# Transposition by VectorE squares and DRAM instead of DMA transposition, and three more products of halves, in a graph network on one Trainium2 core

## The chip, the core and the metric

The kernel runs on one core of a Trainium2 chip. A core has a matrix engine (TensorE, in the profile PE, its weight loads PEld), a vector engine (VectorE, DVE), a scalar engine (ScalarE, ACT), a general engine (GpSimd, POOL) and a queue that issues DMAs (SyncE, SP). The engines run side by side, each through its own instructions in their order, and wait for one another through semaphores. The metric is the device time of one execution in microseconds.

## What is computed

64 graphs of 256 nodes with 256 features each go through two layers. The first is two graph attentions, a norm, a feed forward of 1024 hidden units with relu and a norm; the second is an attention of 8 heads with one value projection for each value of adj, a norm, a feed forward with gelu and a norm. Cut to what matters:

```python
def gat(h, adj, W, a):                       # twice, W1/a1 and W2/a2
    Wh = h @ W
    e = leaky_relu(Wh @ a[:F] + swapaxes(Wh @ a[F:], 1, 2), 0.2)
    return softmax(where(adj > 0, e, -9e15), axis=1) @ Wh
h = layernorm(x + gat(gat(x, adj, W1, a1), adj, W2, a2))
h = layernorm(h + relu(h @ w_ff1 + b_ff1) @ w_ff2 + b_ff2)
q, k = heads(h @ Wq + bq), heads(h @ Wk + bk)
attn = softmax(q @ k.T / sqrt(32))
out = sum(attn * (adj == r) @ heads(h @ Wv[r] + bv[r]) for r in range(4))
x = layernorm(h + out @ Wo + bo)
return layernorm(x + gelu(x @ W1 + b1) @ W2 + b2)
```

adj holds 0 and 1. The kernel relies on it: it looks at all of adj on the way, and a general version at the end runs only if another value was seen.

## The kernel before

All numbers are float32. A matmul of float32 shows in the profile as two records. The work on one graph is cut into pieces with names such as `F.hk1` or `A.dt10`. The letter ahead of the dot is the stage: L loads, G the two graph attentions and the sum with x, F the first feed forward and the projections, A the attention, T its end, the second feed forward and the store. Three lists written out by hand in the file, `START`, `PERIOD` and `END` (lines 43, 65 and 106), set the order of all pieces. `PERIOD` names every piece once with a lag: in the period of graph b, piece `A.pm00/4` works on graph b - 4. So up to six graphs are under way at once, in a loop that repeats 59 times. The order within an engine is the order of this list; the tile pools and the semaphores add the waits. The DMAs of the loop are all issued by SP, in the order of the list too.

Products are made in two ways. `seven_products` (line 598) multiplies a 2x2 arrangement of blocks with seven block products instead of eight, with differences of the weight blocks made in setup (`half_factors`, line 245) and sums of the left blocks (`add_sums`, line 577, on POOL). Its pieces a to e are matmuls, k1 to k4 evict a block from PSUM, p1 to p3 add a further block to it on DVE (line 638). Both feed forwards' first products, the values v and the second feed forward's second product (line 703, tile fX_c, fY_c, fZ_c) are made so. The first feed forward's second product (`out`, line 683, tile ff_a) and q and k (`project`, line 835) are made the plain way, with eight matmuls of 256 columns for each half of the nodes or features; q and k are evicted by ACT with their bias (line 849).

A tile that is to be multiplied from the other side must be transposed: the normed features y of three norms, and the attention p of each of the 8 heads. `turned` (line 462) does it with the DMA's transposition, which takes 16 bit elements. `dt` issues a DMA transposition of the tile seen as halves of float32 (line 470), `dm` two plain DMAs that bring the halves together on the right partitions (line 478), and `mg` a copy by ACT, or for two of the heads by POOL, that interleaves the 16 bit halves to float32 again (line 485). The results are cols and pm. So y and p are written in an order that suits this (lines 520 and 898).

Elsewhere DVE takes part as follows. `away` (line 740) makes the mask of absent edges from adj; line 743 takes adj's maximum for the look at its values. Line 798 multiplies the projected features by the inverse sums of the softmax (whz). Line 926 masks pm. Line 503 adds the residual at the head of a norm, among others to ff_a. Lines 530 and 537 finish the last norm (res_d). POOL scales p by the inverse sums of the softmax (line 911), makes the roots of the norms (line 515), the residuals (lines 555 and 562) and the sums of blocks (line 585).

Of the kernel before, what the change touches and what calls it, by code (L numbers as in the profile page):

```python
# [43 lines left out]
T.hk3/5 A.ex12/3 F.f0/2 A.mx10/3 T.hd/5 A.pm00/4 G.rsA/1 A.vk4/4 L.xT/0 A.mg02/4 A.dm03/4 T.hp3/5  # L44
F.f1/2 T.raC/5 A.ex10/3 G.nmA/1 T.hp2/5 A.pm02/4 A.mg03/4 A.rz12/3 G.wh0/0 T.he/5 T.ge0/5 L.adj/0
A.pm01/4 T.ge1/5 G.wc0/0 A.sp13/3 A.dt11/3 F.dtA/1 A.pm03/4 T.rbC/5 F.lnB/2 A.sp12/3 A.dm11/3
T.hk4/5 A.dt13/3 A.pm12/4 A.rz10/3 G.wh1/0 T.ge2/5 A.sc0/3 F.rsB/2 A.mx02/3 A.o0/4 F.dmA/1 T.ge3/5
G.wc1/0 F.nmB/2 A.sp10/3 F.raA/1 A.o1/4 A.mx03/3 T.u0/5 A.mx01/3 T.fa/5 A.dt12/3 A.mx00/3 A.ex02/3
A.dm13/3 L.x/0 A.oc0/4 A.oc1/4 F.cA/1 F.dtB/2 T.wo/4 A.dt10/3 G.away/0 G.eA/0 T.u1/5 T.u3/5
A.ex03/3 A.ex01/3 G.lrA/0 F.sA/1 T.fk1/5 F.dmB/2 T.fp1/5 T.fb/5 A.mg11/3 F.ha/1 A.dm10/3 T.lnC/4  # L50
F.hb/1 T.fk2/5 G.adA/0 A.rz03/3 A.rz01/3 T.fc/5 T.rsC/4 T.u2/5 F.hk1/1 F.hk2/1 A.sp01/3 T.nmC/4
F.hc/1 T.fk3/5 F.hp1/1 A.ex00/3 G.exA/0 F.hk3/1 A.va/3 T.dtC/4 A.mg13/3 A.rz02/3 F.cB/2 G.rzA/0
T.fp3/5 A.pm11/3 F.hp3/1 T.fd/5 A.sp02/3 G.gA0/0 F.hd/1 G.wd0/0 F.raB/3 T.fp2/5 A.mg10/3 A.rz00/3
G.gA1/0 A.sp00/3 F.hp2/1 A.vk1/3 T.fe/5 T.fk4/5 A.vb/3 A.vk2/3 G.wd1/0 T.lnD/5 A.pm13/3 F.r0/1
F.he/1 A.dt01/3 G.eB/0 F.k/2 F.q/2 A.vp1/3 F.r1/1 T.dmC/4 G.lrB/0 T.cC/4 A.dm12/3 G.adB/0 F.ke0/2
F.hk4/1 F.ke1/2 A.vc/3 A.vk3/3 A.sp03/3 T.sC/4 A.dm01/3 T.ha/4 F.qe0/2 F.qe1/2 G.exB/0 A.dt00/3
A.dt02/3 T.hk1/4 A.vp3/3 A.sc1/2 T.hb/4 A.vd/3 T.nmD/5 G.rzB/0 F.r2/1 T.hp1/4 A.mx11/2 A.mg01/3
A.mx13/2 A.dt03/3 T.rsD/5 F.rbB/3 A.dm00/3 G.gB/0 T.hk2/4 A.vp2/3 A.pm10/3 T.rbD/5 A.mx12/2 F.r3/1
A.ex11/2 F.rbA/1 A.mg12/3 A.rz11/2 A.dm02/3 G.lnA/0 A.ex13/2 F.sB/2 A.mg00/3 T.out/5 A.rz13/2
A.ve/3 A.sp11/2 T.hc/4  # L60
# [5 lines left out]
G.wh0:0 G.wh1:0 G.wc0:0 L.xT:1 G.away:0 G.wc1:0 G.eA:0 G.lrA:0 S.f0:0 G.adA:0 G.exA:0 G.rzA:0  # L66
G.gA0:0 G.wd0:0 G.gA1:0 G.wd1:0 G.eB:0 G.wh1:1 G.lrB:0 L.adj:1 G.wh0:1 S.f1:0 G.adB:0 G.exB:0
G.wc0:1 G.wc1:1 G.rzB:0 L.xT:2 G.gB:0 G.eA:1 G.away:1 G.lrA:1 S.v0:0 G.lnA:0 G.rsA:0 G.nmA:0
G.adA:1 G.wh0:2 S.f2:0 G.exA:1 L.adj:2 G.rzA:1 F.dtA:0 F.dmA:0 S.q0:0 G.wh1:2 G.gA1:1 S.lw:0
G.gA0:1 G.wc0:2 S.v1:0 G.wd0:1 S.q1:0 G.wd1:1 S.v2:0 F.cA:0 F.sA:0 G.eB:1 F.ha:0 G.lrB:1 F.hk1:0  # L70
S.j1:0 F.hb:0 F.raA:0 F.hk2:0 L.x:1 F.hc:0 F.hk3:0 F.hd:0 G.adB:1 S.lr:0 F.hp3:0 F.hp2:0 S.v3:0
G.exB:1 G.wc1:2 F.r0:0 L.xT:3 G.wh0:3 G.rzB:1 F.he:0 F.r1:0 G.eA:2 F.hp1:0 G.away:2 F.hk4:0
F.rbA:0 F.r2:0 G.gB:1 L.adj:3 G.lnA:1 G.rsA:1 F.r3:0 G.nmA:1 G.lrA:2 F.f0:0 F.f1:0 G.adA:2 F.lnB:0
G.wc0:3 F.rsB:0 G.exA:2 F.dtA:1 G.wh1:3 F.dmA:1 S.l0:0 F.nmB:0 G.rzA:2 F.dtB:0 F.cA:1 G.gA1:2
F.ha:1 G.gA0:2 F.sA:1 F.hb:1 F.hk1:1 F.hk2:1 G.wd0:2 G.wd1:2 F.dmB:0 F.hc:1 G.away:3 F.cB:0 G.eB:2
F.k:0 S.l1:0 G.lrB:2 F.hk3:1 F.ke0:0 L.xT:4 F.hp1:1 F.ke1:0 S.l2:0 F.q:0 F.hd:1 G.wc1:3 G.eA:3
G.adB:2 F.qe0:0 F.hp3:1 F.qe1:0 F.hp2:1 A.sc1:0 G.exB:2 F.he:1 F.r0:1 G.rzB:2 F.r1:1 A.mx10:0
A.ex10:0 A.mx11:0 S.p2:0 S.j2:0 A.ex11:0 F.hk4:1 A.mx12:0 A.rz10:0 A.ex12:0 F.sB:0 F.r2:1 L.x:2
G.gB:2 F.r3:1 A.sc0:0 G.lnA:2 A.mx02:0 A.rz11:0 G.lrA:3 A.sp10:0 A.rz12:0 A.dt10:0 G.rsA:2 G.nmA:2
A.mx00:0 G.adA:3 A.sp11:0 A.mx13:0 F.dtA:2 G.exA:3 F.f0:1 F.raA:1 A.dm10:0 A.dt11:0 A.ex02:0  # L80
F.rbA:1 F.dmA:2 G.rzA:3 A.ex13:0 A.ex00:0 F.cA:2 A.sp12:0 F.f1:1 A.dt12:0 A.rz02:0 A.dm11:0
F.lnB:1 G.gA0:3 G.wd0:3 G.gA1:3 A.mg10:0 G.wh0:4 A.mx01:0 F.rsB:1 G.wc0:4 G.wh1:4 A.vb:0 A.rz13:0
A.sp02:0 A.ex01:0 G.wc1:4 F.nmB:1 L.x:3 G.wd1:3 A.dm12:0 F.sA:2 A.mg11:0 A.rz00:0 F.dtB:1 A.sp00:0
A.dt02:0 F.dmB:1 A.va:0 A.mx03:0 A.vk1:0 A.vk2:0 F.ha:2 F.hk1:2 G.eB:3 F.hb:2 F.hk2:2 A.mg12:0
F.hc:2 A.vc:0 A.dt00:0 A.ex03:0 A.sp13:0 F.hk3:2 F.cB:1 F.hp1:2 A.dm00:0 A.pm10:0 A.rz01:0 F.hd:2
A.dm02:0 A.pm11:0 F.k:1 A.vp1:0 F.hp2:2 F.hp3:2 G.lrB:3 A.vk3:0 F.raA:2 A.dt13:0 A.rz03:0 F.r0:2
F.raB:1 F.r1:2 F.ke0:1 F.q:1 G.adB:3 A.sp01:0 F.qe0:1 A.vp3:0 F.rbB:1 A.vd:0 A.sp03:0 F.ke1:1
L.adj:4 A.dt03:0 F.he:2 A.dt01:0 F.qe1:1 A.vp2:0 G.exB:3 A.pm12:0 G.rzB:3 A.ve:0 F.hk4:2 A.sc1:1
A.mg00:0 A.mx13:1 F.r2:2 A.mx11:1 A.dm03:0 F.rbA:2 F.r3:2 A.ex13:1 A.vk4:0 G.gB:3 A.pm00:0
A.dm01:0 A.mg02:0 A.ex11:1 A.mx10:1 A.dm13:0 A.ex10:1 A.mg03:0 A.rz13:1 G.lnA:3 F.raB:0 A.sp13:1  # L90
A.mg01:0 G.rsA:3 A.mx12:1 A.mg13:0 A.rz11:1 A.rz10:1 G.nmA:3 F.f0:2 A.sc0:1 G.eA:4 A.dt13:1
A.ex12:1 A.pm02:0 A.mx01:1 G.lrA:4 A.sp10:1 F.dtA:3 A.mx03:1 A.pm01:0 A.ex03:1 A.pm03:0 F.f1:2
A.o0:0 A.pm13:0 F.lnB:2 A.rz12:1 F.rbB:0 A.dt10:1 G.away:4 A.ex01:1 A.oc0:0 A.rz03:1 A.o1:0
F.dmA:3 A.va:1 A.oc1:0 A.sp11:1 A.dm13:1 F.rsB:2 A.sp12:1 F.nmB:2 T.wo:0 F.cA:3 A.rz01:1 G.adA:4
A.vk1:1 F.ha:3 G.exA:4 A.dm10:1 F.hk1:3 A.vp1:1 T.lnC:0 F.sA:3 T.rsC:0 A.mx00:1 G.rzA:4 F.hb:3
A.mg10:1 F.hk2:3 T.nmC:0 F.dtB:2 F.hc:3 A.sp01:1 A.mg13:1 A.dt11:1 A.ex00:1 A.dt12:1 G.gA0:4
A.mx02:1 F.sB:1 F.hk3:3 F.dmB:2 F.cB:2 F.hp3:3 A.rz00:1 G.gA1:4 A.dm11:1 F.hd:3 G.wd0:4 A.sp00:1
A.ex02:1 F.hp1:3 G.wd1:4 F.k:2 F.raA:3 A.mg11:1 T.dtC:0 A.rz02:1 A.dm12:1 F.q:2 T.dmC:0 F.hp2:3
F.ke0:2 A.vb:1 F.ke1:2 G.eB:4 F.qe0:2 F.he:3 A.dt01:1 F.qe1:2 A.vk2:1 A.sc1:2 A.dt00:1 G.lrB:4
A.mx11:2 T.cC:0 F.rbA:3 F.hk4:3 G.adB:4 A.ex11:2 A.vc:1 A.sp02:1 F.r0:3 A.mx13:2 T.ha:0 A.vk3:1  # L100
A.sp03:1 G.exB:4 F.r1:3 G.rzB:4 T.hk1:0 A.vp3:1 A.vd:1 A.dm01:1 A.dm00:1 A.ex13:2 A.vp2:1 T.sC:0
T.hb:0 T.hk2:0 A.dt02:1 L.x:4 F.r2:3 A.rz11:2 A.mg00:1 F.r3:3 A.mg12:1 G.gB:4 A.mx12:2 A.sp11:2
T.hp1:0 T.hc:0 A.dt03:1 A.pm10:1 G.lnA:4 A.pm11:1 A.mg01:1 A.ve:1 A.pm13:1 F.sB:2 A.rz13:2
A.dm02:1
""".split()
END = """
G.rsA:-1 A.vk4:-4 F.f0:-2 A.mx10:-3 T.hk3:-5 T.raC:-5 T.hp3:-5 A.dm03:-4 G.nmA:-1 A.pm00:-4
A.ex10:-3 T.hd:-5 T.hp2:-5 A.ex12:-3 A.sc0:-3 A.dt11:-3 A.mx02:-3 A.mg03:-4 A.sp13:-3 A.pm03:-4
A.mg02:-4 A.ex02:-3 A.pm12:-4 T.ge0:-5 F.dtA:-1 A.dt13:-3 T.he:-5 A.pm01:-4 A.pm02:-4 T.ge1:-5
F.f1:-2 F.dmA:-1 A.o0:-4 A.rz12:-3 T.hk4:-5 F.cA:-1 A.sp12:-3 T.ge2:-5 T.rbC:-5 A.oc0:-4 A.mx01:-3  # L110
F.lnB:-2 A.dm11:-3 A.o1:-4 F.rsB:-2 A.dm13:-3 F.sA:-1 A.rz02:-3 T.ge3:-5 F.ha:-1 A.sp02:-3
F.nmB:-2 A.oc1:-4 F.hb:-1 F.hk1:-1 F.raB:-3 A.rz10:-3 T.u0:-5 T.wo:-4 A.dt12:-3 A.mx00:-3
A.mg11:-3 F.hk2:-1 F.hc:-1 T.u2:-5 F.hp1:-1 A.mx03:-3 T.lnC:-4 F.dtB:-2 T.rsC:-4 T.u1:-5 T.nmC:-4
T.fb:-5 T.u3:-5 A.dt02:-3 A.ex01:-3 F.dmB:-2 T.fa:-5 A.ex00:-3 T.fk1:-5 F.hk3:-1 A.sp10:-3
A.ex03:-3 T.fk2:-5 F.cB:-2 F.hd:-1 A.va:-3 F.raA:-1 F.hp2:-1 A.rz01:-3 F.q:-2 A.dm02:-3 A.rz00:-3
F.hp3:-1 A.pm11:-3 A.sp00:-3 A.vk1:-3 T.fc:-5 A.mg02:-3 A.rz03:-3 F.qe0:-2 T.dtC:-4 T.fk3:-5
T.fp1:-5 F.r0:-1 F.k:-2 A.sp01:-3 T.fd:-5 F.qe1:-2 T.fp3:-5 A.mg13:-3 A.vp1:-3 F.ke0:-2 F.ke1:-2
T.fp2:-5 A.pm02:-3 F.he:-1 A.dm12:-3 A.dt10:-3 A.vb:-3 A.sc1:-2 A.sp03:-3 A.vk2:-3 F.r1:-1
T.dmC:-4 A.mx12:-2 T.cC:-4 F.hk4:-1 A.dm10:-3 A.dt00:-3 A.vc:-3 A.vk3:-3 A.vp3:-3 F.r2:-1
A.ex12:-2 F.rbA:-1 A.mx13:-2 T.fe:-5 A.mx11:-2 T.fk4:-5 A.rz12:-2 T.ha:-4 A.mg12:-3 T.sC:-4  # L120
A.dt03:-3 F.r3:-1 A.mg10:-3 A.mx10:-2 A.ex13:-2 A.ex10:-2 A.rz10:-2 F.rbB:-3 T.hk1:-4 A.dt01:-3
A.vd:-3 T.hb:-4 T.raC:-4 T.hk2:-4 A.dm00:-3 A.vp2:-3 A.pm10:-3 T.hp1:-4 F.f0:-1 A.sp12:-2 T.lnD:-5
A.mg00:-3 T.hc:-4 A.dm01:-3 A.ex11:-2 A.sc0:-2 T.hk3:-4 T.hd:-4 A.rz13:-2 A.dm03:-3 A.pm12:-3
A.sp10:-2 A.rz11:-2 A.pm13:-3 A.mg03:-3 A.ve:-3 A.sp11:-2 A.dt12:-2 A.mx01:-2 T.hp2:-4 T.hp3:-4
# [63 lines left out]
def binary(ctx: ExitStack, tc: tile.TileContext, t, most, out: bass.AP):  # L188
# [56 lines left out]
    def half_factors(name, width, block):  # L245
# [4 lines left out]
        for at, c, h in ((0, 0, 0), (5, 0, 1), (1, 1, 0), (2, 1, 1)):  # L250
            src = block(c, h)
            to = f[:, at, :]
            if len(src.shape) == 3:
                to = to.rearrange("p (f d) -> p f d", f=src.shape[1])
# [1064 lines left out]
```

## Time and profile before

| What | Value |
|---|---|
| median of three runs | 3073.11 us (3071.72 to 3075.26) |
| span of the profiled execution | 3073.1 us |
| PE busy | 97% of the span, 23270 records |
| DVE, ACT, POOL busy | 83%, 83%, 71% |
| share of the DMA engines in the middle of the run | 0.79, at 148 GB/s |
| TensorE clock granted | 0.994 of full speed in the mean |

The first line of the profile's page gives each engine's busy time. The chain of waits goes back from the last instruction to whatever released it, step by step. A line of the windows gives start and end of a stretch, its length, and then for PE, PEld, DVE, ACT and POOL the busy time and, in brackets, the number of instructions, last the granted clock, the share of the DMA engines and GB/s. A line of the timeline has start and length, then engine, line, operation and what is written from what. An instruction's length overlaps the start of the next one on its engine a little, so that work is better counted from start to start.

### The profile page before, as it was taken

The numbers are of one execution on the slowest core, as the hardware profiler recorded it, in microseconds if no ns is written. First come the engines' busy times: TensorE is split into PE (matmuls) and PEld (weight loads), VectorE is DVE, ScalarE is ACT, GpSimd is POOL, SyncE is SP. The second block draws the span as 40 slices with busy tenths as digits, with TensorE's granted clock in tenths as the row PEclk, the third lists the DMA queues.
The fourth block names the chain that finished last, engine by engine and source line by source line (L and its number), as shares of the span: only waits on it lengthen the run. The fifth ranks groups of instructions, "written<-read, shape, count | busy, mean of one in ns | idle before, by whom it ended". The sixth has DMA issues, their size and how long they took to land.

```text
span 3073.1 us, 68797 instructions
## 1 busy us (share of the span) xinstructions
PE 2985.9 (97%) x23270; PEld 2612.4 (85%) x23270; DVE 2539.8 (83%) x5740; ACT 2556.6 (83%) x5822; POOL 2176.7 (71%) x3057
## 2 busy tenths in 40 slices
PE   7999999999999999999999999999999999999996
PEld 6788888888888888888888888888888888888885
DVE  5788888888888888888888888888888888888865
ACT  2788888888888888888888888888888888888884
POOL 4777777777777777777767777777777777777675
PEclk9999999999999999999999999999999999999999
DMA  6787877879778788777867778878787788788794
GB/s 161 126 160 143 151 152 144 149 146 151 149 147 152 145 148 150 150 143 148 153 143 150 149 142 152 152 140 151 152 145 149 151 145 148 148 151 147 142 146 77
DMA packets 1023941, 449.40 MB, mean 146 GB/s; under 512 B 771008, under 2 KB 1021888, under 8 KB 1023584
## 3 DMA queue, kind: packets, MB, share of 16 engines
q1 hardware_dynamic: 1022048, 442.43, 77.0%
q8 instruction: 187, 3.06, 0.5%
q0 software_dynamic: 976, 1.72, 0.4%
q14 instruction: 170, 1.39, 0.2%
q10 hardware_dynamic: 560, 0.79, 0.1%
HBM read 58.87 MB, written 16.78 MB: 25 GB/s over the span
## 4 chain that ended last, share of the span: by engine, by line
PE 84%; DVE 11%; DMA 2%; issue 1%; ACT 1%; POOL 0%; SPq 0%; DVEq 0%; POOLq 0%; ACTq 0%
PE ff_a L687 14%; PE fX_c L703 7%; PE o L936 7%; PE hX_a L662 7%; PE hX_c L662 5%; DVE res_d L530 5%; PE gat_b L804 4%; PE gat_a L804 4%; PE k L839 4%; PE q L839 4%; PE hY_a L662 4%; PE wh L748 4%; PE fY_c L703 4%; PE wo L955 3%; PE vX L852 3%; PE sc L884 2%
## 5 line engine op out<-in xcount | busy, mean ns | idle before, releaser
L485 ACT COPY pm<-halves_p 128x1024 uint16<-128x1024 uint16 x384 | 520.1, 1357 | 43.2 <-DMA halves_p<-pairs_p 43.1
L687 PE MATMUL ff_a<-w_L_gnn_w_ff,hid_a 128*128 128x256 f32 x2048 | 463.0, 379 | 0.2 <-ACT hid_a L679 0.2
L687 PEld LDWEIGHTS ff_a<-w_L_gnn_w_ff,hid_a 128*128 128x128 f32 x2048 | 379.7, 190 | 47.3 <-ACT hid_a L679 0.6
L926 DVE SCALAR_TENSOR_TENSOR pm<-away,pm 128x512 f32<-128x512 uint8 x512 | 407.3, 806 | 3.7 <-ACT pm L485 2.5
L936 PE MATMUL o<-pm,v 128*32 128x256 f32 x4096 | 234.9, 381 | 0.7 <-DVE pm L926 0.7
L585 POOL TENSOR_TENSOR S_c<-cols_c 128x128 f32<-128x128 f32 x128 | 59.3, 463 | 246.1 <-ACT cols_c L485 246.1
L703 PEld LDWEIGHTS fX_c<-f_L_gnn_W,hid_c 128*128 128x128 f32 x1536 | 196.6, 192 | 35.8 <-ACT oT L947 23.9
L679 ACT ACTIVATE hid_a<-hid_a,col_L_gnn_b_ff 128x256 f32<-128x256 f32 x512 | 225.1, 503 | 0.1
L679 ACT ACTIVATE hid_c<-hid_c,col_L_gnn_b 128x256 f32<-128x256 f32 x512 | 218.5, 497 | 4.8 <-DVE hid_c L638 2.0
L703 PE MATMUL fX_c<-f_L_gnn_W,hid_c 128*128 128x128 f32 x1536 | 209.9, 280 | 3.2 <-ACT hid_c L679 1.6
L936 PEld LDWEIGHTS o<-pm,v 128*32 128x32 f32 x4096 | 126.2, 110 | 98.4 <-POOL rstd_b L515 18.9
L485 POOL COPY pm<-halves_p 128x1024 uint16<-128x1024 uint16 x128 | 172.4, 1347 | 12.8 <-DMA halves_p<-pairs_p 12.7
L530 DVE SCALAR_TENSOR_TENSOR res_d<-acc_c,mv_d,row_L_gnn_g 128x256 f32<-128x256 f32 x128 | 170.8, 1373 | 0.0
L804 PE MATMUL gat_b<-whz_B,s_B 128*128 128x256 f32 x512 | 127.3, 391 | 36.3 <-DVE hid_c L638 33.1
L804 PEld LDWEIGHTS gat_b<-whz_B,s_B 128*128 128x128 f32 x512 | 91.7, 189 | 71.0 <-DVE hid_c L638 56.8
L662 PEld LDWEIGHTS hX_c<-cols_c,f_L_gnn_W 128*128 128x128 f32 x1024 | 133.7, 191 | 17.4 <-ACT cols_c L485 8.0
L884 PE MATMUL sc<-kT,qT 32*128 32x256 f32 x2048 | 147.7, 400 | 0.0
L662 PE MATMUL hX_c<-cols_c,f_L_gnn_W 128*128 128x128 f32 x1024 | 135.9, 276 | 8.3 <-ACT cols_c L485 7.2
L662 PEld LDWEIGHTS hY_c<-S_c,f_L_gnn_W 128*128 128x128 f32 x1024 | 126.1, 193 | 19.9 <-issue 19.6
L662 PE MATMUL hY_c<-S_c,f_L_gnn_W 128*128 128x128 f32 x1024 | 142.7, 283 | 0.0
L804 PE MATMUL gat_a<-whz_A,s_A 128*128 128x258 f32 x512 | 137.3, 392 | 5.2 <-DVE whz_A L798 4.9
L662 PEld LDWEIGHTS hX_c<-S_c,f_L_gnn_W 128*128 128x128 f32 x1024 | 133.7, 191 | 9.2 <-ACT hid_c L673 2.1
(2758 smaller groups left out, 9567.5 us busy)
## 6 DMA issues: line engine op xcount, KB each, us to landing
halves_p<-pairs_p SPq DMA_DIRECT2D x1024, 128.0 KB, 3.3
xT<-in_xT SPq DMA_DIRECT2D x64, 256.0 KB, 3.3
adj<-in_adjT SPq DMA_DIRECT2D x64, 256.0 KB, 3.4
x<-in_x SPq DMA_DIRECT2D x64, 256.0 KB, 4.4
halves_y_a<-pairs_y_a SPq DMA_DIRECT2D x128, 128.0 KB, 3.5
halves_y_y<-pairs_y_y SPq DMA_DIRECT2D x128, 128.0 KB, 3.1
halves_y_c<-pairs_y_c SPq DMA_DIRECT2D x128, 128.0 KB, 3.2
out<-res_d SPq DMA_DIRECT2D x64, 256.0 KB, 2.2
```

The lines of the kernel that those rows point to most:

```text
L485: copy(into().bitcast(U16).rearrange("p (n s) -> p s n", s=2), t["halves"].rearrange("p s k q -> p s (k q)"),)
L530: nc.vector.scalar_tensor_tensor(tiles["res"][:, i, :], tiles["acc"][:, i, :], tiles["mv"][:, i, 0:1], rows[last[0]], ALU.subtract, ALU.mult,)
L662: nc.tensor.matmul(ps[:, f * P : (f + 1) * P], weights()[0][:, factor, f * P : (f + 1) * P], left, start=start and f == 0, stop=f == FC // ...
L679: nc.scalar.activation(tiles["hid"][:, f, :], tiles["hid"][:, f, :], func, bias=b1[:, f : f + 1])
L687: nc.tensor.matmul(tiles["ff"][:, i, :], tiles["hid"][:, f, nodes(i)], weights()[2][:, f, :], start=(f == 0), stop=(f == FC - 1),)
L703: nc.tensor.matmul(ps, left[:, f, :], weights()[2][:, factor, f * P : (f + 1) * P], start=start and f == 0, stop=f == FC // 2 - 1, skip_gr ...
L748: nc.tensor.matmul(t["whp", j], tiles["xT"][:, c, nodes(j)], wx[:, c, :], start=(c == 0), stop=(c == KC - 1),)
L804: nc.tensor.matmul(ps, t["s"][:, j, nodes(i)], t["whz"][:, j, :width], start=(j == 0), stop=(j == NT - 1),)
L839: nc.tensor.matmul(t[key + "p"][:, o, :], w[:, c, nodes(o)], tiles["cols"][:, c, :], start=(c == 0), stop=(c == KC - 1),)
L884: nc.tensor.matmul(t["sc", g, hh][:, i, :], qkv["q"][hd, g, nodes(i)], qkv["k"][hd, g, :], start=True, stop=True,)
L926: nc.vector.scalar_tensor_tensor(pm[:, 1, :], tiles["away"], 0.0, pm[:, 0, :], ALU.is_equal, ALU.mult)
L936: nc.tensor.matmul(ps[hh * DH : (hh + 1) * DH, :], qkv["v"][:, j, d0 : d0 + DH], t["pm", (g, hh)][:, r, j * N : (j + 1) * N], start=(r == ...
```

## The change

The change has several parts. It replaces the DMA transposition by DVE's transposition in squares of 32x32 float32 (`dt`), a plain DMA of the tile to DRAM (`dm`) and four plain DMAs back, one for each quarter of the partitions (`mg`); heads are handled in pairs, so that there are four tiles p of 1024 columns in place of eight of 512. The copies that joined halves are gone. The orders within y, p, pm, e, s, away, and of x and adj in DRAM follow from this. The first feed forward's second product becomes a `seven_products` like the second's, and q and k together become one. whz is multiplied on ACT. The look at adj becomes a square on ACT with a sum (of (2 adj - 1) squared, which is the number of entries if all are 0 or 1). The tiles pm have 4 buffers of double size. Weights are loaded in more pieces. And the three lists are new; `PERIOD` reaches to lag 6.

```diff
-    def turned(do, stage, key, name, src, into, engine):
+    def turned(do, stage, key, name, width, src, into, out=None):
...
-        def turn():
-            t["pairs"] = work.tile([P, 2, 4, P], U16, tag="pairs", name=f"pairs_{name}", bufs=3)
-            nc.sync.dma_start_transpose(
-                out=t["pairs"].rearrange("p c k q -> p (c k) q"),
-                in_=src().rearrange("p c a b n -> p (c a b n)").bitcast(U16),
-            )
+        def squares():
+            rows = src()
+            t["squares"], to = out() if out else (rows, rows)
+            nc.vector.transpose(to, rows)
+
+        def leave():
+            t["far"] = far.tile([4, 32, 4, width], F32, tag=f"far{width}", name=f"far_{name}", bufs=8)
+            nc.sync.dma_start(
+                out=t["far"].rearrange("a c b n -> (a c) (b n)"), in_=t["squares"]
+            )
 
-        def part():
-            t["halves"] = work.tile([P, 2, 4, P], U16, tag="halves", name=f"halves_{name}", bufs=3)
-            for c in range(2):
+        def back():
+            to = into()
+            for b in range(4):
                 nc.sync.dma_start(
-                    out=t["halves"][c * 64 : (c + 1) * 64].rearrange("p s k q -> p s (k q)"),
-                    in_=t["pairs"][:, c].rearrange("p k q -> p (k q)"),
-                )
-
-        def join():
-            copy = nc.scalar.copy if engine == "ACT" else nc.gpsimd.tensor_copy
-            copy(
-                into().bitcast(U16).rearrange("p (n s) -> p s n", s=2),
-                t["halves"].rearrange("p s k q -> p s (k q)"),
-            )
+                    out=to[b * 32 : (b + 1) * 32],
+                    in_=t["far"][:, :, b, :].rearrange("a c n -> c a n"),
+                )
...
         def into():
-            tiles["cols"] = work.tile([P, KC, N], F32, tag="cols", name=f"cols_{name}", bufs=3)
-            return tiles["cols"].rearrange("p k n -> p (k n)")
+            cols = work.tile([P, KC * N], F32, tag="cols", name=f"cols_{name}", bufs=3)
+            if pairs:
+                tiles["cols"] = cols.rearrange("p (n k) -> p k n", k=KC)
+            else:
+                tiles["cols"] = cols.rearrange("p (a t k r) -> p k t a r", a=4, t=NT, k=KC)
+            return cols.rearrange("p (a n) -> p a n", a=4)
...
-            nc.vector.tensor_reduce(most[:, b : b + 1], tiles["adj"].bitcast(U32), AX.X, ALU.max)
+        def binary_or_not():
+            nc.scalar.activation(
+                tiles["adj"], tiles["adj"], AF.Square, bias=minus_one, scale=2.0,
+                accum_out=most[:, b : b + 1],
+            )
...
-                nc.vector.tensor_scalar_mul(
-                    t["whz"][:, j, :width], t["wh", step][:, j, :width], rz[:, j : j + 1]
+                nc.scalar.activation(
+                    t["whz"][:, j, :width], t["wh", step][:, j, :width], AF.Copy,
+                    scale=rz[:, j : j + 1],
                 )
...
-        def project(w, key):
-            t[key + "p"] = mm_tile(f"{key}_{b}")
-            for o in range(KC):
-                for c in range(KC):
-                    nc.tensor.matmul(
-                        t[key + "p"][:, o, :], w[:, c, nodes(o)], tiles["cols"][:, c, :],
-                        start=(c == 0), stop=(c == KC - 1),
-                    )
+        def natural(ap):
+            return ap.rearrange("p (a t r) -> p t a r", a=2, t=NT)
+
+        def into(ps, factor, left, start):
+            for n, (w, right) in enumerate(((wq, natural(left)), (wk, left))):
+                nc.tensor.matmul(
+                    ps[:, nodes(n)], w[:, factor, :], right,
+                    start=start and n == 0, stop=n == 1, skip_group_check=True,
+                )
...
+        def begin_keys(i, h, ps):
+            for to, src, bias in zip(keys(i, h), both(ps), (bq, bk)):
+                nc.scalar.activation(to, src, AF.Identity, bias=bias[:, h : h + 1])
+
+        def add_keys(i, h, ps):
+            for to, src in zip(keys(i, h), both(ps)):
+                nc.vector.tensor_tensor(to, to, src, ALU.add)
...
-        feed_forward(do, "F", f"a{b}", a, lambda: ff0, "r", AF.Relu, seven=False)
-        y = layernorm(do, "F", "B", f"b{b}", lambda: (a["ff"], a["res"]))
-        to_columns(do, "F", "B", f"y{b}", y, "ACT")
+        feed_forward(do, "F", f"a{b}", a, lambda: ff0, "r", AF.Relu)
+        y = layernorm(do, "F", "B", f"b{b}", lambda: (a["ff"],))
+        to_columns(do, "F", "B", f"y{b}", y, pairs=True)
```

`far` is a pool in DRAM with 8 buffers of each size. In the order of the built program, one period holds 39 DMAs on SP: 7 stores to DRAM, 28 loads from it, and those of x, its transpose, adj and the output.

## The prediction

> **What bounds the kernel now.** I read the page's first part, then a table of windows for the steady stretch, then the chain of waits.
>
> ```profile
> span 3073.1 us, 68797 instructions
> PE 2985.9 (97%) x23270; PEld 2612.4 (85%) x23270; DVE 2539.8 (83%) x5740; ACT 2556.6 (83%) x5822; POOL 2176.7 (71%) x3057
> ...
> PE 84%; DVE 11%; DMA 2%; issue 1%; ACT 1%; POOL 0%; SPq 0%; DVEq 0%; POOLq 0%; ACTq 0%
> ```
>
> TensorE (PE) carries the chain. In the chain's list the same pieces come back every 46.494 us (the output products of attention at 320.35, 366.85 and 413.35), so 64 graphs take 64 x 46.494 = 2975.6 and filling, draining and setup the other 97.5. The profiled span, 3073.1, equals the median of the runs, 3073.11, so no correction is needed between them.
>
> The window holds fifty periods (start and length; busy PE, weight loads, VectorE, ScalarE, GpSimd):
>
> ```profile
> 325.40:2650.00 2324.60, 2296.54 (x18101) 2016.21 (x18100) 1974.71 (x4451) 1999.63 (x4551) 1670.50 (x2351) 1.00 0.79 148
> ```
>
> Per period: PE 45.93 of 46.49, VectorE (DVE) 39.49, ScalarE (ACT) 39.99, GpSimd (POOL) 33.41; the granted clock is 1.00. PE idles 0.56. Where, the chain in order of time shows (start, length, who):
>
> ```profile
> 1006.24 3.46 PE ff_a L687 x16
> 1009.70 0.89 PE hX_c L662 x8
> ...
> 1039.26 1.73 PE k L839 x8
> 1040.99 1.73 PE q L839 x8
> 1042.72 0.45 PE vX L852 x2
> ...
> 1043.72 0.42 DVE v L638
> 1044.14 2.72 DVE res_d L530 x2
> ```
>
> Two things are to be seen. PE's rate: 16 records of 256 columns in 3.46 are 216 ns each, 8 of 128 columns in 0.89 are 112 ns. And the one piece of DVE work that hurts PE: res_d at L530, 1.36 each, although L537 does the same kind of work on the same width in 0.40. The timeline gives DVE's other prices as start to next start:
>
> ```profile
> 1001.90 0.68 DVE L891 TENSOR_REDUCE am_(1, 1)_11853<-sc 128x2 f32<-128x512 f32 x1
> 1002.50 0.67 DVE L891 TENSOR_REDUCE am_(1, 3)_11857<-sc 128x2 f32<-128x512 f32 x1
> 1003.10 0.40 DVE L638 TENSOR_TENSOR v<-v,vX 128x256 f32<-128x256 f32 x1
> 1003.42 0.68 DVE L926 SCALAR_TENSOR_TENSOR pm<-away,pm 128x512 f32<-128x512 uint8 x1
> 1004.03 0.87 DVE L537 SCALAR_TENSOR_TENSOR res_d<-res_d,rstd_d,row_L_gnn_beta 128x256 f32<-128x256 f32 x2
> 1004.82 0.68 DVE L891 TENSOR_REDUCE am_(1, 2)_11877<-sc 128x2 f32<-128x512 f32 x1
> ```
>
> A 512-wide instruction takes 0.60 of the engine, a 256-wide one 0.32 to 0.40. All DVE terms below are such means over the fifty periods.
>
> **PE, per graph.** ff_a loses 32 records of 216 ns (6.91) and gains 7 products x 4 blocks x 2 records = 56 of 112 ns (6.25): -0.65. q and k lose 16 records (3.46) and gain 7 x 2 x 2 = 28 of 112 ns (3.13): -0.33. Nothing else on PE changes in count, so its work falls from 45.93 to 44.95. With today's idle 0.56 the period is 45.51, a gain of 0.98 x 64 = 63 us. That is all the change can give; the rest decides whether it arrives. One doubt on PE: cols of y becomes a tile with a step of two elements, read by 12 of the new records and by v's weight loads. No row has such a step; from below 0, from above the price of 256 columns, whose bytes it spans: 12 x 0.104 = +1.25. I take 0, by the nearest row: the broadcast operand at L764 runs at 110 ns (two records in 0.22).
>
> **ACT, per graph.** Nine join copies go: 6 on pm at 1.254 and three on cols at 1.21 to 1.35, together -11.28. Four whz multiplies come (copies of that width, L758, take 0.27 to 0.36: +1.3), adj's squares with their accumulator (a 512-wide copy, L673, 0.50, plus a read of 0.11), and eight 128-wide key and query evictions for four 256-wide ones (0.36 to 0.44 each; between half price, +0.1, and full, +1.6). ACT falls to 31 or 32 of 45.5. It gives the room away; nothing waits for it.
>
> **POOL, per graph.** Two join copies go (-2.62) and four sums of ff_a's hidden blocks come, 4 x 1.28 = +5.13. The scaling of p, 16 x 0.52, keeps count and width. 33.41 becomes 35.9, 79% of the period: not the bound, but it is beside DVE more often.
>
> **DVE, per graph: the step that decides.** Work now 39.50 (start to next start, idle left out). Gone: adj's maximum 0.60, whz 0.81 + 0.69, ff_a's residual addition 0.70 (it rides in the eviction): -2.80. Added: ff_a's evictions, 4 x 0.241 + 3 x 0.228 (the acc_c rows) = +1.65; additions into q and k, 6 x 0.228 = +1.37 (the same rows). And the transposes, three 512 wide and four 1024 wide. No row has one. From below, 22 pieces of 256 columns at 0.27, the shortest whz multiply: 5.9; from above, away at L740, 1.29 per 512: 14.2. I take the reductions at L891, one source, same width, 0.60 per 512, with 1.05 ns for each further column (0.33 at 256, 0.60 at 512): 3 x 0.60 + 4 x 1.14 = +6.36. Sum: 39.50 - 2.80 + 1.65 + 1.37 + 6.36 = **46.08**, which is more than PE's 45.51.
>
> In that sum, 3.0 are collisions: res_d 2 x (1.367 - 0.40) = 1.93 and the pm products 8 x (0.735 mean - 0.602 median) = 1.06. When res_d ran at 1044.14 POOL was in two 512-wide sums (1043.89 to 1046.58); at 1004.03, with POOL idle, the same form took 0.40. Without collisions DVE needs 43.1, with half of them 44.6, plus 0.6 for some 17 hand-overs of 35 ns between dependent instructions. So up to 1.8 of collision PE stays the bound; with all 3.0 DVE needs 46.7. In the built program's order res_d again stands just behind the instruction that releases POOL's rstd_d, and two sums of hidden blocks follow that on POOL, so its collision probably stays; the pm products stand next to POOL's scaling of p.
>
> [...]
>
> **DMA and the SP queue.** Now a tile is transposed (3.6 us to landing), copied in two halves (3.3), joined by a copy (1.35): 8.3. Then: DVE 1.14, to DRAM (out, 256 KB, lands in 2.2; p's 512 KB between 2.2 and 4.4), back in four pieces of the size of halves (3.3): about 7.7. So lateness is equal. SP's issuing: 11 transposes at 1.25 and 22 halves at 0.59 fall away (26.7), 7 stores and 28 loads come, 35 x 0.41 to 0.60 (out and halves) = 14 to 21. But a load waits for its store to land with all of SP's queue behind it; the order has five such places without other work between, 5 x 2.2 to 4.4 = 11 to 22. SP then stands at 27 to 45 of 45.5, now at 29 plus waits. I take the middle and no cost; at the upper end p's tiles would be late for the pm products. Packets become 1 KB and 512 B where 771008 of 1023941 are under 512 B now, for the same 146 GB/s, so the engines' share (0.79) should fall.
>
> [...]
>
> **Fixed part.** Setup adds differences on POOL: four of 1.34 (L259 rows) and eight of 128 columns at 0.46, 9.0 in all, during a fill in which POOL was busy 20.4 of the first 46.5. Between 0 and 9.0; I take half: 97.5 + 4.5 = 102.
>
> **The sum.** PE 44.95 + idle 0.56 = 45.51; because DVE's idle falls from 7.0 to under 1, I add 0.2, about a third of a second wait like today's: 45.7. 64 x 45.7 + 102 = **3027 us**. Faster.
>
> **Rivals.**
> - DVE is the bound, slower. Mechanism: res_d, pm and the new transposes on an engine with no slack. Price: 46.08 + 0.6 = 46.7 as it stands, up to 48 if POOL's extra 2.5 collide as well: 64 x 46.7 + 102 = 3091 to 3174. It decides from 46.42 (3073 less 102, over 64). For: the sum itself. Against: collisions depend on the order, which is new.
> - PE alone: the new order avoids collisions, idle stays: 64 x 45.51 + 97.5 = 3010, and 2974 without idle.
> - Transposes near the upper price (14.2): DVE 54, 64 x 54.5 + 102 = 3590. For: no row; against: the reduction rows.
> - SP's queue or PE's stepped operand ends the period: +1.25 on PE gives 46.76, so does SP if its worst case of 45.4 is late by as much: 64 x 46.76 + 102 = 3095.
> - The work moved off ACT was free, so the change does nothing: 3073. PE's count of records speaks against it.
>
> **Chances.** Forecast region 3015 to 3066: 0.33. PE alone, 2974 to 3015: 0.21. Nothing, within 6 us: 0.05. DVE bound: 0.30. SP or PE's step: 0.06. Dear transposes: 0.05. Faster 0.54, same 0.05, slower 0.41; 0.2% is about what a measurement of this kernel can tell from none. Range 2980 to 3150: it leaves out the dear transposes, the top of the DVE case and a little below. Both signs carry weight; the forecast's own range is 3015 to 3066.
>
> **What would show it.** Right: ff_a's output and q, k in records of 112 ns, PE busy near 45 per period, a period of 45.5 to 46.2, DVE over 95% of it, a 1024-wide transpose near 1.14, no copies of pm on ACT. Wrong: transposes over 1.5 each, res_d or pm above 1.3 in the mean, PE idle over 1.5 per period on DVE, or stores that land later than 4.4.

## The result, and the profile after

The changed kernel takes 3190.1 us (median of four, 3188.8 to 3191.5), the kernel before 3072.5 in the same comparison: 1.038 times as long, 95% interval 1.037 to 1.040. The forecast was 3027 in a range of 2980 to 3150, so it was wrong in sign and in range. The profiled execution spans 3187.0 us.

The first lines of the page and the shares of the chain of waits, after the change:

```profile
span 3187.0 us, 75089 instructions
PE 3002.4 (94%) x25574; PEld 2673.8 (84%) x25574; DVE 2907.3 (91%) x6644; ACT 2053.8 (64%) x5886; POOL 2454.5 (77%) x3198
...
DVE 48%; POOL 17%; PE 16%; issue 15%; DMA 1%; SPq 1%; ACT 1%; POOLq 0%; DVEq 0%; ACTq 0%
```

PE had 84% of the chain and has 16%. DVE leads, but POOL has a sixth, and 15% is "issue", time for which the profile names nobody. So there is no new single bound: the chain walks from engine to engine.

From the starts of the same instruction in successive graphs the period is 48.38 us (before 46.49): 64 x 48.38 = 3096, and 91 remain for filling, draining and setup (before 97.5). The whole loss is in the period. Work (from start to next start, idle time left out) and idle time per period, worked out over the steady stretch:

| | before | after |
|---|---|---|
| PE work / idle | 45.93 / 0.56 | 46.20 / 2.17 |
| DVE work / idle | 39.5 / 7.0 | 45.1 / 3.27 |
| ACT work | 40.0 | 32.1 |
| POOL work / idle | 33.4 / 13.1 | 37.7 / 10.7 |

No engine is full. DVE's groups by line and form (busy time, mean ns of one, idle time before them) show what became of it, first in the kernel before, then after:

```profile
L779 DVE SCALAR_TENSOR_TENSOR e_B<-s_B 128x512 f32<-128x512 f32 x64 | 45.0, 703 | 7.2 <-ACT s_B L772 7.2
...
L511 DVE TENSOR_SCALAR var_c<-mv_c 128x2 f32<-128x2 f32 x64 | 10.8, 169 | 2.2
```
```profile
L516 DVE STREAM_TRANSPOSE p<-p 128x1024 f32<-128x1024 f32 x256 | 309.7, 1227 | 63.6 <-POOL p L999 63.4 <-issue 0.3
...
L840 DVE SCALAR_TENSOR_TENSOR e_B<-s_B 128x512 f32<-128x512 f32 x64 | 102.2, 1598 | 3.4 <-ACT s_B L832 3.4
...
L553 DVE TENSOR_SCALAR var_c<-mv_c 128x2 f32<-128x2 f32 x64 | 35.3, 552 | 2.2
```

The transposition is as cheap as forecast. But e_B, which nobody touched in kind, takes 1.60 us in place of 0.70, and var_c, which adds a constant to two elements, 0.55 in place of 0.17. The timeline of one such place shows why:

```profile
1009.80 1.26 POOL L643 TENSOR_TENSOR H_a<-hid_a 128x512 f32<-128x512 f32 x1 [1.54 <-PE fY_c L756]
...
1010.63 0.47 DVE L553 TENSOR_SCALAR var_c<-mv_c 128x2 f32<-128x2 f32 x1
...
1014.42 1.28 POOL L643 TENSOR_TENSOR hid_a<-hid_a 128x512 f32<-128x512 f32 x1
...
1014.57 1.69 DVE L840 SCALAR_TENSOR_TENSOR e_B<-s_B 128x512 f32<-128x512 f32 x1
```

var_c starts at 1010.63 and ends at 1011.10, just after POOL's sum (1011.06). e_B starts at 1014.57, POOL's sum ends at 1015.70, and 0.56 later e_B is done, as if it had stood until POOL was through. These sums, H_a and hid_a, are the four that the seven products of ff_a brought. Not every meeting is with one of them. var_a ends with a sum of cols_c (at 1025.12), which the kernel before has as well:

```profile
1024.66 0.46 POOL L643 TENSOR_TENSOR S_c<-cols_c,S_c 128x128 f32<-128x128 f32 x1
...
1024.67 0.48 DVE L553 TENSOR_SCALAR var_a<-mv_a 128x2 f32<-128x2 f32 x1
```

In the steady stretch of the kernel before, no POOL instruction ran beside e_B or var_c (none of 50 each). In that of the changed kernel one did in all 48: e_B ended 0.56 after POOL's sum, var_c 0.02 after it (medians). DVE's TENSOR_REDUCE shows nothing of the kind: am and gm, 512 wide, take 0.67 to 0.69 in all 480 cases of that stretch, also in the 135 that started while POOL had 0.2 or more left of a TENSOR_TENSOR of over 1.1 us. An experiment below puts this form in the place of var's.

### The profile page after: what moved, and what is told of

Same layout as the page of the kernel before. It is cut to its first block, busy times and chain, and to the rows that moved or that the text cites. A ratio compares the mean times of both kernels' runs of the same rounds, so it can differ in the third digit from the quotient of the medians.

```text
span 3187.0 us, 75089 instructions
## 1 busy us (share of the span) xinstructions
PE 3002.4 (94%) x25574; PEld 2673.8 (84%) x25574; DVE 2907.3 (91%) x6644; ACT 2053.8 (64%) x5886; POOL 2454.5 (77%) x3198
## 4 chain that ended last, share of the span: by engine, by line
DVE 48%; POOL 17%; PE 16%; issue 15%; DMA 1%; SPq 1%; ACT 1%; POOLq 0%; DVEq 0%; ACTq 0%
POOL p L999 10%; DVE p L516 6%; POOL H_c L643 5%; PE fX_a L756 4%; PE gat_b L872 3%; DVE hid_c L701 3%; DVE e_B L840 3%; DVE e_A L840 2%; DVE y_a L562 2%; DVE y_c L562 2%; DVE stats_a L550 2%; DVE pm L1013 1%; DVE v L701 1%; DVE gat_b L545 1%; DVE stats_c L550 1%
## 5 line engine op out<-in xcount | busy, mean ns | idle before, releaser
L516 DVE STREAM_TRANSPOSE p<-p 128x1024 f32<-128x1024 f32 x256 | 309.7, 1227 | 63.6 <-POOL p L999 63.4
L756 PE MATMUL fX_a<-f_L_gnn_w_ff,hid_a 128*128 128x128 f32 x1536 | 209.3, 279 | 59.4 <-DVE acc_a L767 56.1
L756 PEld LDWEIGHTS fX_a<-f_L_gnn_w_ff,hid_a 128*128 128x128 f32 x1536 | 191.2, 191 | 75.8 <-POOL hid_c L643 64.3
L736 ACT COPY hid_a<-hX_a 128x512 f32<-128x512 f32 x192 | 113.7, 592 | 133.1 <-PE hX_a L725 132.9
L736 ACT COPY hid_c<-hX_c 128x512 f32<-128x512 f32 x192 | 111.2, 579 | 126.3 <-PE hX_c L725 126.3
L557 POOL TENSOR_TENSOR rstd_b<-var_b,neghalf 128x2 f32<-128x2 f32 x64 | 45.0, 703 | 179.7 <-DVE var_b L553 176.7
L855 ACT ACTIVATE s_B<-e_B,gm_B 128x256 f32<-128x256 f32 x128 | 59.6, 471 | 179.3 <-DVE gm_B L844 176.1
L966 PEld LDWEIGHTS sc<-kT,qT 32*128 32x128 f32 x2048 | 97.5, 184 | 69.4 <-PE hY_a L725 35.1
L643 POOL TENSOR_TENSOR H_a<-hid_a 128x512 f32<-128x512 f32 x64 | 81.7, 1277 | 86.4 <-PE fY_c L756 81.5
L725 PE MATMUL hX_a<-cols_a,f_L_gnn_w_ff 128*128 128x128 f32 x1024 | 136.8, 277 | 3.7 <-DMA cols_a<-far_y_a 2.8
```

The source lines that it names most:

```text
L516: nc.vector.transpose(to, rows)
L643: engine.tensor_tensor(to[i], one, other, op)
L725: nc.tensor.matmul(ps[:, f * P : (f + 1) * P], weights()[0][:, factor, f * P : (f + 1) * P], left, start=start and f == 0, stop=f == FC // ...
L736: nc.scalar.copy(hidden(i, h), ps.rearrange("p (f n) -> p f n", n=P))
L756: nc.tensor.matmul(ps, left[:, f, :], weights()[2][:, factor, f * P : (f + 1) * P], start=start and f == 0, stop=f == FC // 2 - 1, skip_gr ...
L966: nc.tensor.matmul(t["sc", g, hh][:, i, :], qkv["q"][hd, g, nodes(i)], qkv["k"][hd, g, :], start=True, stop=True,)
```

## The experiments

Theory A: DVE's total is the bound, so the time follows DVE's work. Theory B: the hand-over from POOL's scaling of p to DVE's transposition. Theory C: the trip through DRAM. Theory D: PE itself is slower. Diffs are cut; "..." marks what was left out. Ratios are to the kernel before, with 95% intervals; "after" stands for the changed kernel's 3190.

**Scaling p on ACT.**

```diff
-                nc.gpsimd.tensor_scalar(
-                    quarters(h, i), quarters(h, i), t["rz", h][:, i : i + 1], 1.0,
-                    ALU.mult, ALU.mult,
+                nc.scalar.activation(
+                    quarters(h, i), quarters(h, i), AF.Copy, scale=t["rz", h][:, i : i + 1]
                 )
```

> The scaling of p (16 instructions per graph, 10.4 us per period on POOL as it ran) goes to ACT, which is busy for only 31 of 48.4 us. Nothing else changes. Theory A (DVE's total: its 45.2 of work and 3.3 of gaps fill the 48.4 us period): only those collisions with POOL go that the scaling causes, pm 8 x (0.65 - 0.60) = 0.4 and little more, so 3150 to 3185. Theory B (the in-order loop POOL scales p, then DVE transposes: DVE waits 63 us in all for the scaling and POOL carries 17% of the chain): the wait of 1.0 per period goes and POOL's sums come earlier, period 46.2 to 47.2, so 3050 to 3120. Theory C (DVE's new waits lie in the trip through DRAM) and theory D (PE itself is slower): no change, 3180 to 3200.

Measured: 3258 (1.061, 1.059 to 1.062). Slower still, which no theory had. POOL's work falls to 27, but DVE still waits 60 us for p in the steady stretch, now from ACT, and ACT enters the chain with 18%. Freeing an engine is worth nothing when the wait moves to another one's queue. Theory B falls in this form. Where the further 68 us come from was not traced.

**No transposition of p.**

```diff
-            nc.vector.transpose(to, rows)
+            if out:
+                nc.vector.transpose(to, rows)
```

> The four transpositions of p on DVE are left out (4 x 1.16 = 4.6 us per period), the trip through DRAM stays; p thus arrives untransposed. Theory A: DVE's work falls from 45.2 to 40.6, PE becomes the bound with 45 of work and 0.5 to 1.0 of idle: 64 x 45.5 to 46.0 + 90 = 3000 to 3035. Theory B: the hand-over loses its wait and 1.2 of latency, period 46 to 47, 3035 to 3100. Theory C: p leaves 1.2 us earlier, at most 3120 to 3190. Theory D: 3180 to 3200.

Measured: 3161 (1.029, 1.028 to 1.031). DVE's work falls by 3.1 us per period (of the 4.6 removed, var_c and away lost 1.2 again, since they now met POOL), the period by only 0.46, and DVE's idle grows from 3.3 to 5.9. Theory A falls: DVE's total is not the bound. In the chain PE (49%) and DVE (41%) take turns: 24 us of PE from hX_c to wo, then DVE with short pieces of PE between, and in DVE's part stand e_B (1.62) and var_c (1.24).

**Six products of seven.**

```diff
         def e():
-            product(ps["X"], 6, left(1, 1), False)
+            return
```

> The seventh product (piece e) of all seven_products is left out, so that the results lack a term: PE loses 4 x 8 records of 112 ns, 4 of 112 and 2 of 216 per graph, 4.5 us of 45; no other engine loses or gains an instruction. Theory A and B (DVE, or the loop of DVE and POOL, bounds): PE's 16% of the chain give back at most 0.5 per period, 3150 to 3195. Theory D (PE bounds, by narrower products and a stepped operand): period 44 to 45, 2900 to 2980. Theory C: no change.

Measured: 3273 (1.064, 1.061 to 1.066). With 4.5 us less for PE at full clock (2.6 less as it ran, 43.6 against 46.2) the kernel is slower by 82. Theory D falls. Why slower is taken up below.

**A cheaper first instruction on res_d.**

```diff
-                nc.vector.scalar_tensor_tensor(
+                nc.vector.tensor_scalar(
                     tiles["res"][:, i, :], tiles["acc"][:, i, :], tiles["mv"][:, i, 0:1],
-                    rows[last[0]], ALU.subtract, ALU.mult,
+                    1.0, ALU.subtract, ALU.mult,
```

> The first of the two instructions on res_d (L571, subtract the mean, multiply by gamma; two sources from SBUF, 2 x 1.08 us as it ran beside POOL) becomes one with a single source and no gamma: gamma of the last norm is left out of the result. This takes work away from DVE far from the transpositions. Theory A: DVE loses 2.15 - 2 x 0.30 = 1.55 per period, so 3080 to 3105. Theory B: DVE's wait for the scaling of p takes most of it back, 3150 to 3190. Theories C and D: no change.

Measured: 3180 (1.035, 1.033 to 1.037). The edit missed its aim: the pair went from 2.13 to 2.02 us, not to 0.60. The TENSOR_SCALAR with its single source took 1.01 in the mean, as if it waited for POOL as well (in the changed kernel the instruction in its place meets POOL in all 96 cases of the steady stretch). It tells nothing between A and B, but it led to the next theory, F: the fixed order makes a loop through PE, DVE and POOL, and what DVE loses to POOL inside this loop lengthens the period. Theory G, as a rival: ACT's exponentials wait for the store of an earlier p (53 us in all), since p has two buffers.

**No epsilon, halves, a third buffer, and all three.**

```diff
-            nc.vector.tensor_scalar_add(tiles["var"], mv[:, :, 1], EPS)
...
-            nc.gpsimd.tensor_tensor(tiles["rstd"], tiles["var"], neghalf, ALU.pow)
+            nc.gpsimd.tensor_tensor(tiles["rstd"], tiles["mv"][:, :, 1], neghalf, ALU.pow)
```

> The four small DVE instructions that add the norm's epsilon to the variances (var, L553) are left out; the roots on POOL read the variances themselves, so epsilon is left out of the result. As they ran they took 0.49, 0.38, 0.28 and under 0.1 us per period, where the same took 0.08 each in the kernel before. Theory A (DVE's total): -1.2 per period, 3110. Theory F (the order's loop through PE, DVE and POOL, stretched by what DVE loses to POOL inside it; var_c and var_a are in the chain): -0.8 to -1.2, 3110 to 3140. Theory G (ACT's exponentials of p wait for the store of an earlier p, since p has two buffers, and all that stands behind them on ACT with them): 3175 to 3195.

```diff
-            add_sums(nc.gpsimd, blocks, tiles["H"], [n])
+            for half in range(2):
+                f = slice(2 * half, 2 * half + 2)
+                add_sums(nc.gpsimd, [x[:, f] for x in blocks], [x[:, f] for x in tiles["H"]], [n])
```

> POOL's eight 512-wide sums of hidden blocks per graph become sixteen of 256: POOL's work grows by about 8 x 0.2 = 1.6 of 10.7 spare, while a DVE instruction that meets one waits for at most 0.7 in place of 1.3. Theory F: e_B (1.67), e_A (1.25) and the var instructions lose 0.3 to 0.6 in all, 3145 to 3175. Theory A: the same size, through DVE's sum. Theory G: 3185 to 3230, since POOL comes later to the scaling of p.

```diff
-                    [P, 2 * NT * N], F32, tag="p", name=f"p_{b}_{g}{hh // 2}", bufs=2
+                    [P, 2 * NT * N], F32, tag="p", name=f"p_{b}_{g}{hh // 2}", bufs=3
...
```

> p has three buffers in place of two; the room is made by one gamma row for all four norms and the last beta, so their values are wrong while every instruction stays. Theory G: ACT's wait for the store of p (0.85 per period, 53 us in all) goes, and what is behind it on ACT comes earlier: 3095 to 3140. Theories A and F: 3175 to 3195.

> The three edits together: no epsilon in the roots, one gamma row for all and a third buffer for p, sums in halves. Theory F alone: 3080 to 3120. Theory G alone: 3095 to 3140. Both together: the period falls to 46.0 to 46.8, where PE's 45 of work and 1.0 to 1.8 of waits set it: 3035 to 3090. Theory A: DVE's work falls to 43.3 and the time with it by 1.8 x 64, 3070.

Measured: without the var instructions 3094 (1.007, 1.005 to 1.009); with halves 3119 (1.015, 1.013 to 1.017); with a third buffer 3191 (1.039, 1.037 to 1.040); all three 3072 (1.000, 0.999 to 1.001). Theory G falls: with the third buffer ACT's wait for the store is gone and the time stays. Theory F holds, and its numbers were too small. Four instructions that should cost 0.08 each were worth 1.5 us of period (96 us over 64 graphs), more than the 1.25 they took as they ran. Halves make POOL's work *longer* (37.7 to 39.8) and the kernel 72 us faster; e_B falls from 1.67 to 0.77 and res_d from 2.13 to 1.35. But halves act on both engines. In the changed kernel the weight loads of fX_a waited 64 us in all for POOL's sums, and its matmuls then 56 us for acc_a, which stands shortly behind e_B on DVE; with halves it is 6 and 4. So this run alone does not tell DVE's delay from POOL's.

**Is it the instruction or the meeting?** The same addition as a reduction over variance and epsilon (mv has a third column for it and is now one tile for each norm, in place of a new one for each graph), then with halves of the sums, then also with halves of the residual additions:

```diff
...
-            nc.vector.tensor_scalar_add(tiles["var"], mv[:, :, 1], EPS)
+            nc.vector.tensor_reduce(tiles["var"], mv[:, :, 1:3], AX.X, ALU.add)
```
```diff
-            nc.gpsimd.tensor_tensor(tiles["res"], tiles["res"], over_nodes(b), ALU.add)
+            for i in range(NT):
+                nc.gpsimd.tensor_tensor(
+                    tiles["res"][:, i, :], tiles["res"][:, i, :], rows[b], ALU.add
+                )
```

> Epsilon comes back, and with it four small DVE instructions per graph, in another form: a reduction that adds the variance and an epsilon kept beside it. So DVE has as many instructions as in the changed kernel, but the form TENSOR_SCALAR, which met POOL's long sums, is replaced by TENSOR_REDUCE, of which no row shows a stretched one. If the meeting with POOL was the price (theory F): 4 x 0.1 = 0.4 per period at most over the version without the instruction, 3085 to 3125. If the instruction as such, with its place in the chain, was the price: 3170 to 3190.

> The reduction in place of the addition, and POOL's sums of hidden blocks in halves; nothing is left out. Theory F: PE becomes the bound again, at its 45.9 of work and 0.4 to 0.9 of waits: period 46.3 to 46.8, 3062 to 3095, level with the kernel before. If the two edits cured the same loss, no better than the better of them alone, 3085 to 3120.

> As the run with the reduction and the sums in halves, and POOL's three 512-wide additions to the residuals in halves as well (about 3 x 0.15 more work on POOL). Theory F: what is left of long meetings (e_A 1.14, res_d) shrinks a little, but PE bounds, so between -20 and +5 against that run: 3050 to 3090. If POOL's load counts (39.6 of 46.3), 3080 to 3110.

Measured: 3131 (1.019, 1.018 to 1.021), 3088 (1.005, 1.003 to 1.006) and 3066 (0.997, 0.996 to 0.998). As many instructions on DVE as in the changed kernel, in a form that does not wait (0.16 in all four norms): the reduction alone gives 59 of the 96 us that leaving the instruction out gave (3131 is a little above theory F's range). So the larger part is the meeting. In the third of these versions, called cured from here, the same two groups stand at:

```profile
L850 DVE SCALAR_TENSOR_TENSOR e_B<-s_B 128x512 f32<-128x512 f32 x64 | 49.8, 778 | 4.6 <-ACT s_B L842 4.6
...
L558 DVE TENSOR_REDUCE var_c<-mv_C 128x2 f32<-128x4 f32 x64 | 10.0, 157 | 2.2
```

and its chain belongs to PE again, in the profiled execution, the fastest of its seven runs:

```profile
PE 81%; DVE 10%; POOL 3%; DMA 2%; issue 2%; ACT 1%; SPq 1%; DVEq 0%; POOLq 0%; ACTq 0%
```

**The opposite dose.**

```diff
-            for i in range(NT):
-                nc.gpsimd.tensor_tensor(
-                    tiles["res"][:, i, :], tiles["y"][:, i, :], rows[g], ALU.mult
-                )
+            nc.gpsimd.tensor_tensor(tiles["res"], tiles["y"], over_nodes(g), ALU.mult)
```

> The opposite dose, on the changed kernel: POOL's three products with gamma (2 x 256 columns each) become one of 512 each. POOL has three instructions less and about 0.2 to 0.4 us less work per period, and DVE's work is the same, but a DVE instruction that meets such a product waits for up to 1.3 in place of 0.7. Theory F: slower, by 0.1 to 0.6 per period, 3195 to 3230. If POOL's or DVE's total counted: 3165 to 3190.

Measured: 3192 (1.038, 1.037 to 1.040), no change: a miss. e_B, e_A and the var instructions stay within 0.03 of what they were. In the trace these products stand beside none of those DVE pieces. A longer POOL instruction cost nothing where none of them met it.

**What bounds the cured version, and a control.** The edits of the second and third experiment on the cured version, and the halves (of POOL's sums and residual additions, without the reduction, since the four var instructions take 0.08 each there) on the kernel before:

> On the version with the reduction and POOL's sums and additions in halves, the seventh product of all seven_products is left out again (results lack a term; PE loses 4.5 us of nominal work per graph). The same edit made the changed kernel slower by 82 us. Theory F with PE as the bound of the cured version: PE gives back part of the 4.5, until DVE's 42.9 of work and 3 of waits for PE bind, period 44 to 45.4: 2920 to 3020. If a loop through DVE and POOL still bounds: 3060 or more, slower again.

> On the same version, DVE's four transpositions of p are left out (4.6 us per period of DVE's work; p arrives untransposed). If PE bounds the cured version, DVE's total is worth almost nothing: 3045 to 3070. If DVE's load of 42.9 of 45.8 still costs through its queue: 3000 to 3040.

> A control: the kernel before with POOL's four sums of hidden blocks and three residual additions in halves, nothing left out. DVE has 7.0 us of waits per period there and PE 0.56; the meetings with POOL cost DVE 3 us off the path. Theory F: within 3068 to 3080, and at best the 0.56 of PE's idle, 3040. So what the cured version gains on the kernel before belongs to the change. If it gains 10 us or more here, the edit, not the change, beats the kernel before.

Measured: six of seven 3090 (1.004, 1.003 to 1.006), no transpositions 3036 (0.986, 0.984 to 0.989), the kernel before with halves 3038 (0.988, 0.986 to 0.990). Three things follow.

The control is the most sobering: the cure helps the kernel before as well, by 36 us. PE's 0.56 of idle there is gone. Its windows line, then that of the cured version:

```profile
325.40:2650.00 2324.60, 2324.60 (x18319) 2044.80 (x18319) 1970.79 (x4516) 2022.10 (x4611) 1769.71 (x2735) 1.00 0.82 150
```
```profile
325.40:2650.00 2324.60, 2314.87 (x20125) 2099.56 (x20127) 2174.30 (x5221) 1622.37 (x4655) 2018.60 (x3044) 1.00 0.47 150
```

In the first PE is busy in all of the 2324.60 us. So the change, cured, does not beat the kernel before with the same cure: 3066 against 3038. What it still lacks was not tried out further. The two profiled periods are nearly equal (45.92 cured, 45.87 before), and of the 12.7 us between these two executions (3046.5 and 3033.8) ten lie outside the 64 periods (108 against 98). But the cured version's profiled execution is the lowest of its runs (3048 to 3069, the next 3062), so a typical one is not on record.

Without p's transpositions 30 us go, though PE leads. DVE's load on its queue may be the reason; it was not shown.

The lighter PE loses 24 us again. By its expectation a loop through DVE and POOL then bounds; the chain (PE 41%, DVE 27%, POOL 14%) fits that in part, and the clock comes on top. The windows of the cured version without the seventh product (length, five engines, clock), and PE's timeline at the same place:

```profile
1014.00:1016.00 2.00, 1.94 (x30) 1.01 (x22) 1.23 (x2) 1.54 (x5) 2.00 (x5) 1.00 0.34 120
1016.00:1018.00 2.00, 0.16 (x1) 0.19 (x2) 1.97 (x6) 1.75 (x5) 2.00 (x4) 1.00 0.00 0
1018.00:1020.00 2.00, 2.00 (x6) 1.62 (x6) 0.90 (x2) 0.98 (x4) 0.40 (x1) 0.55 1.02 406
1020.00:1022.00 2.00, 2.00 (x10) 1.73 (x10) 0.70 (x1) 0.98 (x4) 0.00 (x0) 0.59 0.72 226
```
```profile
1014.79 1.15 PE L976 MATMUL sc<-kT,qT 32*128 32x256 f32 x16
1017.84 3.41 PE L1055 MATMUL wo<-w_L_gnn_Wo,oT 128*128 128x256 f32 x8 [1.90 <-ACT whz_A L875]
```

PE, done early, waits 1.90 us for ACT; then its granted clock is 0.50 from 1018.21 to 1021.62 (so the last two windows show 0.55 and 0.59), and wo, on the chain, takes 3.41 in place of 1.99 (median of the 64 in the changed kernel). On the changed kernel without the seventh product the clock fell like this in 22 of the 47 periods of the steady stretch, after a gap of 1.9, and its mean was 0.98. This explains how less work can cost time, but it is not all of the 82 us: periods with such a fall last 50.4 in the mean, the others still 49.6, against 48.4 in the changed kernel. What makes those longer stays open.

## Why the prediction was wrong, step by step

- **PE's records**: 112 ns as forecast, the stepped operand free (k's four records on cols of y take 0.45). But the saving of 0.98 is mis-sized. In the cured version, where PE hardly idles, q and k take 3.55 in place of 3.13, ff_a 6.4 in place of 6.25, the scores 0.2 more than before, and PE's work is 45.72, 0.21 under before. So PE had some 13 us to give (64 x 0.21), not the 63 that the prediction called all that the change can give.
- **ACT**: 32.1 work, as forecast. **POOL**: 37.7 against 35.9; the scaling of p kept count and width, but its 16 instructions went from 0.52 to 0.65 each: three in four take 0.45, the rest 1.2, with pm or res_d of DVE beside them.
- **Transpositions**: 1.16 and 0.63 us start to start, 6.5 in sum against 6.36. Right.
- **DVE's sum**: 45.1 against 46.08, so even too high: away found no POOL instruction running at its start in its new place (0.33 in place of 1.28), and res_d and pm lost less (2.13 and 5.17). That the sum came within 1.0 is partly luck: these three are 2.3 lower than assumed, and 2.4 of meetings at e_B, e_A and var, which it did not have, stand against them.
- **DMA and SP**: p's store lands in 3.1, the loads in 2.9, the share of the DMA engines fell to 0.44. Right; DVE's pm waited for loads 2.1 us in all.
- **Fixed part**: 91 against 102. In the cured version the same subtraction gives 108 (3046.5 less 64 x 45.92), so it is not shown that the setup is free.
- **The failing step** is the one after the sum: "So up to 1.8 of collision PE stays the bound", and with it "I add 0.2". It compared totals of two engines and took the larger. The runs showed that neither total sets the period: DVE idles 3.27 (forecast 0.6) and PE 2.17 (0.76) while both are nearly full, because each waits for the other in a fixed order. And it took the meetings with POOL from the old rows (res_d, pm), although it had counted POOL's four new sums of 1.28. In the built order two of these stand beside var_c and e_B, which take 0.41 and 0.98 longer than before. Beside e_A (0.53), var_a (0.31) and var_d (0.20) stand sums and residual additions that the kernel before has too: there it is the new order that brought the meeting. e_B, e_A, var_c and var_a are on the chain. The prediction's own sign of being wrong, PE idle over 1.5, came true.
- **The rival "DVE is the bound"** (3091 to 3174) named DVE without slack and came nearest in time, but leaving out DVE's work (the second experiment) showed that it is not the total either. That the change does not beat the kernel before even when cured was in no case of the prediction.

## What to carry to other kernels

When two engines are both above 90% (here 94% and 91%, with 2.17 and 3.27 us of idle per period) and hand work to and fro in a fixed order, the larger total is only a floor: add the hand-overs of the loop, and look in the built order for what stands beside the loop's instructions. Between DVE and POOL count meetings by their place, not by their sum; a longer total of shorter POOL instructions can be faster (39.8 in place of 37.7 per period, and 72 us less, here), and so can another form of a small DVE instruction (four of 0.08 undisturbed, in a form that does not wait, were worth 0.9 us per period here). Before crediting a cure to a change, apply it to the kernel before.

## What the runs showed of the hardware

In the changed kernel a DVE TENSOR_SCALAR on two elements with one source was lengthened beside POOL's sum, as the 512-wide e_B was: var_c beside H_a took 0.55 in place of 0.17 us busy, e_B 1.60 in place of 0.70; var_b, with no POOL instruction beside it, kept 0.17. In the run with the reduction alone TENSOR_REDUCE takes 0.16 in all four norms, in three of them (var_a, var_c, var_d) beside the same POOL sums; var_b meets none in either kernel.

After a PE gap of 1.90 us the granted clock was 0.50 for 3.41 us (the rows above, of the cured version without the seventh product); on the changed kernel without the seventh product it was so after gaps of 1.9 in 22 of 47 periods. In the trace of the changed kernel without the seventh product, all starts of such stretches are whole multiples of 3.41 us apart. So are those of the seven stretches at 0.50 in the kernel before, and of the seven in the changed kernel, all of them in filling and draining. On the grid of the run without the seventh product the 3.41 us ahead of each of the 22 in the steady stretch held all of a gap of 1.9; of some 660 others one held as much idle time, and the clock stayed. So in that run it seems to matter whether a gap falls whole between two marks of the grid or across one.
